# Turned rows and sums of values asked for at other steps in a fused stack of four graph attention layers

## The chip, the cores and the metric

The kernel runs on one core of a Trainium2 chip, in one launch. The metric is the device time of an execution in microseconds; the time of a kernel is the median of several executions. The engines of the core are named as in the profile: PE is TensorE (matmuls; PEld is its loading of weights), DVE is VectorE, ACT is ScalarE, POOL is GpSimd, and SP is SyncE, which only issues DMA transfers.

## The reference

3327 rows of 256 features pass through four layers over one adjacency matrix of 3327 x 3327 (0 or 1). Every layer is attention over the neighbours, a residual and a normalisation of rows:

```python
x = _layernorm(x + _L0_gnn_ref(x, adj, Wq, Wk))          # cosine attention on x itself
x = _layernorm(x + _L1_gnn_ref(x, adj, W, a))            # GAT: elu(att @ (x @ W))
x = _layernorm(x + _L2_gnn_ref(x, adj, Wq, bq, Wk, bk, Wv, bv))  # elu(softmax(q @ k.T / 16) @ v)
x = _layernorm(x + _L3_gnn_ref(x, adj, W0, W1, a1, W2, a2, W3, a3))  # x @ W0, then three GATs
```

with, for a GAT layer,

```python
h = x @ W
e = leaky_relu((h @ a[:D])[:, None] + (h @ a[D:])[None, :])
att = softmax(where(adj > 0, e, MASK_VAL), axis=1)
out = elu(att @ h)
```

## The kernel before

**Tiling.** The rows are padded to 3328, that is 26 row tiles of 128, and the columns of the attention matrix are cut into seven blocks: six of 512 (four row tiles each) and block 6 of 256 (two row tiles). The program has six stages, called layers in the code: "0", "1" (GAT), "2", and "3a", "3b", "3c" (the three GATs of the last layer). Its main loop runs over steps (layer, block b, row tile j). A step makes the attention weights e of row tile j against the columns of block b, and multiplies them with the values v of row tile j into the block's accumulators `po` in PSUM. After the 26 steps of a block, `finish` (L790) turns the accumulators into rows of the next layer.

**Weights.** In a GAT layer e comes from ScalarE (`re`, L599) and VectorE (L607) and needs no matmul. In layers "0" and "2" it needs the scores `ps` (TensorE, L444 and L506), an exponential (ScalarE, `ex`, L453 and L514) and the mask (VectorE, L433). Weights are made two steps ahead of their products (`LA = 2`), in five buffers. The mask of a block, 1664 KB in DRAM, is fetched at step j = 8 for the next block (L370), into two buffers; it can only be fetched when the last e that reads the old mask is made.

**Products.** Ordinarily they are one matmul for each group of 128 columns (L1163). In layer "2" and in blocks 1 to 5 of layer "0" they are done for pairs of row tiles with seven products in the manner of Strassen (L704). These use sums of weights (`ssum`, L645 on, VectorE) and sums of values, `tsum`: `combine` (L625) makes the sums of values of pair p once, on VectorE, and writes them to DRAM (`t_d`, 256 KB a pair, L636); `fetch_tsum` (L640, issued on SP at L642) brings them back into one of three buffers when a pair's weights are made. In layer "2" the values themselves are only made while layer "1" ends and layer "2" begins: those of row tiles 24 and 25 (pair 12) last, because the mean of all rows goes into the very last one (`Sum.close`, L783).

**Turned rows.** A GAT projects its rows after the attention, for which TensorE needs them transposed. `turn` (L752) does so: ScalarE copies the rows into two planes of 16-bit halves (`planes`, L759), SP issues a DMA transpose (`turned`, L762), and after `steps` yields VectorE copies the halves to their places (L769). Then come the projections `pproj` (L924) on TensorE, ELU (ScalarE L937 and L938, VectorE L944 and L953), statistics (L802, L803), the reciprocal square root `rsqrt` (L132 to L144, eleven small operations on VectorE), and the normalised rows o (L982). In layer "1" those are written to DRAM (`x_d`, L994) and turned a second time, into `FT`; from FT TensorE makes layer 2's values with `pv` (L1011), and `combine` follows. FT is also what layer 2's scores read. `block2` (L458) prepares a block of layer 2's scores: `pgq` (L465), `gT` (L472), its largest magnitudes gm (L480), a sum over partitions `pn` (L488), and from that, by another rsqrt, a bound `off` (L496).

**Order.** `finish` is a generator. It is advanced once a step (`advance`), and what is left of it at j = 20 is flushed, so each `yield` spreads its work over one more step of the next block. The rows of block 5 are thus worked on during block 6, whose steps are about half as long, and those of block 6 in the first block of the next layer. The first four steps are laid down in the order written; from there on a scheduler orders the instructions of each engine by its own model of time, with the order of emission as priority. On each engine instructions then run in that order.

## Time and profile before

| | |
|---|---|
| time, median of 3 runs | 2385.57 us (2384.24 to 2386.73) |
| the profiled execution's own time | 2386.53 us |
| its span | 2384.5 us |
| TensorE's granted clock, mean | 0.996 of full speed |
| DMA, mean | 89 GB/s |
| `turned`: DVE idle until the transpose has landed | 26.2 us in 32 waits |
| `tsums`: fetches | 156, of 256.5 KB |
| mask fetches of 1664 KB | 30 |

The span reaches from the first to the last instruction that the profiler saw; the execution's own time has 2.0 us around it. A wait is idle time of an engine together with what ended it. Idle time of an engine that doesn't set the pace costs nothing by itself: VectorE's 26.2 us before the turned rows are only of account where TensorE stops in turn. In a line of the timeline the first two columns are start and duration in us, then engine, line, operation, output<-inputs, and how many instructions of the kind run there; a bracket gives the idle time ahead of it and what ended that.

### The profile page before, as it was taken

To read this page: it belongs to the slowest core of one execution; us is meant where nothing else is said; L and a number is where in the kernel's file an instruction comes from. 1 tells how busy PE (TensorE), PEld (TensorE's weight loads), DVE (VectorE), ACT (ScalarE), POOL (GpSimd) and SP (SyncE) were. 2 spreads that over 40 slices of the span, in tenths; PEclk is the share of its full clock that TensorE was granted. 3 is DMA by queue.
4 is the path that set the end of the run, shared out by engine and by line. 5 is a ranking of instruction groups with operands and counts; after the bars stand their busy time and mean duration, and the time that the engine had idled before them with its cause. 6 is when DMAs were issued, how large, how long until landed. Compare 5 with 4: busy or idle time off the path is not lost.

```text
span 2384.5 us, 33058 instructions
## 1 busy us (share of the span) xinstructions
PE 2348.6 (98%) x11911; PEld 1915.7 (80%) x11911; DVE 1615.5 (68%) x4340; ACT 1215.7 (51%) x1982; POOL 14.2 (1%) x91
## 2 busy tenths in 40 slices
PE   9999999999999999999999999999999999999997
PEld 6687777888888776667767798888888888888886
DVE  7789999866676657567567585556656555655665
ACT  5666666665555422222222255565655555655554
POOL 0000000000000000000000000000000000000000
PEclk9999999999999999999999999999999999999999
DMA  7556555523222322212212221221211111132121
GB/s 230 169 164 193 187 183 185 164 89 87 73 75 64 102 54 91 73 59 87 72 51 73 78 92 47 67 56 31 73 49 43 43 59 50 45 98 69 60 61 27
DMA packets 146233, 212.83 MB, mean 89 GB/s; under 512 B 76062, under 2 KB 100885, under 8 KB 141461
## 3 DMA queue, kind: packets, MB, share of 16 engines
q1 hardware_dynamic: 145796, 210.45, 29.3%
q8 instruction: 94, 1.54, 0.3%
q14 instruction: 71, 0.57, 0.1%
q10 hardware_dynamic: 272, 0.26, 0.1%
HBM read 165.70 MB, written 28.19 MB: 81 GB/s over the span
## 4 chain that ended last, share of the span: by engine, by line
PE 64%; DVE 2%; DMA 1%; ACT 1%; issue 0%; DVEq 0%; POOL 0%; POOLq 0%; SPq 0%; ACTq 0%
PE po L1163 37%; PE ps L506 12%; PE po L704 11%; PE pproj L924 3%; PE pgq L465 1%; DMA turned<-planes 1%; ACT re L599 1%; DMA t_d<-tsum 0%; PE pv L1011 0%; DVE e L607 0%; DVE ejunk L533 0%; DVE pT L769 0%; ACT planes L759 0%; DMA u<-s_d 0%; DVE v L953 0%
## 5 line engine op out<-in xcount | busy, mean ns | idle before, releaser
L1163 PE MATMUL po<-v,e 128*128 128x257 f32 x5720 | 1275.7, 381 | 2.8 <-ACT p L882 2.0
L1163 PEld LDWEIGHTS po<-v,e 128*128 128x128 f32 x5720 | 1083.2, 190 | 178.1 <-issue 14.6
L599 ACT ACTIVATE re<-u,nrh,th 128x512 f32<-128x512 f32 (+1 forms) x728 | 558.8, 783 | 488.6 <-DVE e L607 485.8
L607 DVE SCALAR_TENSOR_TENSOR e<-re,rh,mask 128x512 f32<-128x512 f32 (+1 forms) x728 | 515.1, 711 | 389.5 <-PE po L1163 366.3
L433 DVE SCALAR_TENSOR_TENSOR e<-ex,mask 128x512 f32<-128x512 f32 (+1 forms) x364 | 236.5, 655 | 183.0 <-ACT ex L514 156.7
L506 PE MATMUL ps<-gT,ft 128*128 128x512 f32 (+1 forms) x728 | 307.7, 563 | 0.0
L514 ACT ACTIVATE ex<-ps,off 128x512 f32<-128x512 f32 (+1 forms) x182 | 119.4, 657 | 360.3 <-PE ps L506 332.3
L704 PE MATMUL po<-tsums,ssum 128*128 128x128 f32 (+1 forms) x1794 | 250.1, 275 | 3.0 <-DMA tsums<-t_d 1.6
L704 PEld LDWEIGHTS po<-tsums,ssum 128*128 128x128 f32 x1794 | 224.4, 192 | 5.4 <-DMA tsums<-t_d 2.4
L704 PEld LDWEIGHTS po<-v,e 128*128 128x128 f32 x1196 | 169.7, 191 | 71.6 <-issue 54.3
L506 PEld LDWEIGHTS ps<-gT,ft 128*128 128x128 f32 x728 | 131.9, 190 | 113.6 <-issue 110.7
L704 PE MATMUL po<-v,e 128*128 128x129 f32 x1196 | 183.2, 275 | 0.2 <-DVE e L433 0.2
L453 ACT ACTIVATE ex<-ps 128x512 f32<-128x512 f32 (+1 forms) x182 | 102.9, 565 | 119.3 <-PE ps L444 107.3
L444 PE MATMUL ps<-ft,ft 128*128 128x512 f32 (+1 forms) x312 | 142.9, 566 | 0.8 <-ACT ft L356 0.7
L405 DVE CUSTOM_DVE_ANT_0 acc<-acc,stage 128x1024 uint16<-128x1024 uint16 (+1 forms) x168 | 111.5, 663 | 13.0 <-DMA stage<-in_adj_a 8.3
L704 PE MATMUL po<-v,ssum 128*128 128x128 f32 x598 | 92.3, 275 | 0.0
L704 PE MATMUL po<-tsums,e 128*128 128x128 f32 x598 | 92.2, 275 | 0.0
L397 ACT ACTIVATE mask<-pos 128x1024 uint8<-128x1024 bf16 (+1 forms) x87 | 86.6, 995 | 2.4
L396 ACT ACTIVATE pos<-stage 128x1024 bf16<-128x1024 int32 (+1 forms) x87 | 85.8, 987 | 2.7 <-DVE e L433 2.7
L924 PE MATMUL pproj<-w_l_w,pT 128*128 128x256 f32 x312 | 80.2, 381 | 3.8 <-DVE pT L769 2.2
L704 PEld LDWEIGHTS po<-v,ssum 128*128 128x128 f32 x598 | 79.4, 192 | 0.1
L704 PEld LDWEIGHTS po<-tsums,e 128*128 128x128 f32 x598 | 79.3, 192 | 0.1
(191 smaller groups left out, 1667.9 us busy)
## 6 DMA issues: line engine op xcount, KB each, us to landing
mask<-mask_d SPq DMA_DIRECT2D x30, 1664.0 KB
tsums<-t_d SPq DMA_DIRECT2D x156, 256.5 KB
stage<-in_adj_a SPq DMA_DIRECT2D x78, 512.0 KB
mask_d<-mask SPq DMA_DIRECT2D x6, 1664.0 KB
t_d<-tsum SPq DMA_DIRECT2D x26, 256.5 KB
u<-s_d SPq DMA_DIRECT2D x24, 256.0 KB
mask<-mask_d SPq DMA_DIRECT2D x5, 832.0 KB
v<-in_x SPq DMA_DIRECT2D x26, 128.0 KB
```

The source lines that it names most:

```text
L397: nc.scalar.activation(mask(b, j, 2), t_[:, : 2 * wd], AF.Sign)
L405: nc.vector.tensor_tensor(acc, acc, st[:, h * wd : (h + 1) * wd], ALU.add)
L433: nc.vector.scalar_tensor_tensor(e[:, :wd], t_[:, :wd], 0.0, mask(b, j), ALU.add, ALU.mult)
L444: nc.tensor.matmul(ps[:, :wd], FT[j // 4][:, 0, (j % 4) * P : (j % 4 + 1) * P], FT[b][:, 1, :wd], start=True, stop=True,)
L453: nc.scalar.activation(t_[:, :wd], ps[:, :wd], AF.Exp)
L506: nc.tensor.matmul(ps[:, :wd], FT[j // 4][:, h, (j % 4) * P : (j % 4 + 1) * P], g[:, h, :wd], start=(h == 0), stop=(h == 1),)
L514: nc.scalar.activation(t_[:, :wd], ps[:, :wd], AF.Exp, bias=off, scale=1.0 / D**0.5)
L599: nc.scalar.activation(t_[:, :wd], self.u[b][:, :wd], AF.Relu, bias=self.nrh[:, j : j + 1], scale=self.th[:, j : j + 1],)
L607: nc.vector.scalar_tensor_tensor(e[:, :wd], t_[:, :wd], self.rh[:, j : j + 1], mask(b, j), ALU.add, ALU.mult,)
L704: nc.tensor.matmul(o, x, y, start=(p == 0 and g not in banks[:i]), stop=(p == NT // 2 - 1 and g not in banks[i + 1 :]),)
L924: nc.tensor.matmul(pm[:, :D], pT[:, h, :], w[L.w][:, h, :], start=(h == 0), stop=(h == 1),)
L1163: nc.tensor.matmul(pos[k], es[:, k * P : (k + 1) * P], V[L.i % 2][j], start=(j == 0), stop=(j == NT - 1),)
```

## The change

Sums of values are fetched for the pair at hand and for the one two steps later, with a fourth buffer; pair 12 of layer 2's block 0 is left out of the early fetch. `turn` waits four steps by default instead of three; a GAT's first turn waits seven for block 5's rows instead of five; layer 1's second turn waits six for block 5's rows and four otherwise, instead of three. To make room, two tiles of the start (`count`, `part`) and the mean's row share buffers that other tiles use at other times.

```diff
-    count = const.tile([P, P], F32, name="count")
+    count = work.tile([P, P], F32, tag="sq0", name="count", bufs=1)
...
-    part = const.tile([P, P], F32, name="part")
+    part = work.tile([P, P], F32, tag="sq1", name="part", bufs=1)
...
     def fetch_tsum(key, b, p):
-        t = work.tile([P, 4 * H + 1], F32, tag="tsum", name="tsums", bufs=3)
+        t = work.tile([P, 4 * H + 1], F32, tag="tsum", name="tsums", bufs=4)
...
-    def turn(x4, n, out, steps=3):
+    def turn(x4, n, out, steps=4):
...
         def close(self, v):
...
-            row = work.tile([P, D], F32, tag="mrow", name="mrow", bufs=1)
+            row = work.tile([P, D], F32, tag="elu_e", name="mrow", bufs=2)
...
                     lambda t: pT4[:, :n].bitcast(U16).rearrange(
                         "p k h (i t) -> p t k h i", t=2
                     )[:, t],
-                    5 if b == NB - 2 else 3,
+                    7 if b == NB - 2 else 4,
                 )
...
                     lambda t: FT[b].bitcast(U16).rearrange(
                         "p h (k i t) -> p t k h i", k=4, t=2
                     )[:, t, :n],
+                    6 if b == NB - 2 else 4,
                 )
...
+    fetched = set()
...
     def make(s):
         if s >= len(steps):
             return
         L, b, j = steps[s]
-        if strassen(L, b) and j % 2 == 0:
-            fetch_tsum(L.key, b, j // 2)
+        if j % 2 == 0:
+
+
+            for n in (s, s + 2):
+                if n < len(steps) and not (n > s and steps[n] == (layers[2], 0, NT - 2)):
+                    if strassen(*steps[n][:2]) and n not in fetched:
+                        fetch_tsum(steps[n][0].key, steps[n][1], steps[n][2] // 2)
+                        fetched.add(n)
```

## The prediction

> **What bounds the kernel now.** I read the page's shares of busy time first, then TensorE's list of waits, then the timeline around each wait that the change could touch.

> ```profile
> span 2384.5 us, 33058 instructions
> PE 2348.6 (98%) x11911; PEld 1915.7 (80%) x11911; DVE 1615.5 (68%) x4340; ACT 1215.7 (51%) x1982; POOL 14.2 (1%) x91
> L1163 PE MATMUL po<-v,e 128*128 128x257 f32 x5720 | 1275.7, 381 | 2.8 <-ACT p L882 2.0
> ```

> TensorE is busy for 98% of the span at full clock, and the change removes no matmul. So no edit can bring more than the waits it removes, and any edit can cost a new wait. The list of TensorE's waits (total, times, longest) says what is there to win:

> ```profile
> PE pproj L924 <- DVE pT L769: 3.1, 6, 0.7
> PE po L1163 <- ACT p L882: 2.0, 2, 1.3
> PE po L704 <- DMA tsums<-t_d: 1.6, 1, 1.6
> PE pv L1011 <- DVE ft L769: 1.0, 1, 1.0
> PE pn L488 <- DVE g L485: 0.5, 1, 0.5
> ```

> The edits aim at the first, third and fourth lines: 3.1 + 1.6 + 1.0 = 5.7 us, 0.24% of the span. Everything else they could do is loss. From the timeline, the six waits of pproj are 0.32 at 749.4 us and 0.28 at 1612.8 (ordinary blocks), and 0.71 at 801.1, 0.59 at 1709.9, 0.60 at 2029.3 and 0.59 at 2348.9 (last blocks of layers 1, 3a, 3b, 3c). The one wait of pv is where layer 1 gives over to layer 2. I show that place, all engines, because my forecast hangs on it:

> ```profile
> 813.06 1.38 DVE L982 TENSOR_SCALAR o<-y,st,rstd 128x256 f32<-128x256 f32 x4
> 814.52 1.99 ACT L759 COPY planes<-o 128x1024 uint16<-128x1024 uint16 x2 [0.75 <-DVE o L982]
> 816.54 1.94 SPq L762 DMA_TRANSPOSE turned<-planes  x1
> ...
> 819.16 0.36 SPq L370 DMA_DIRECT2D mask<-mask_d  x1
> ...
> 820.87 1.36 DVE L769 COPY ft<-turned 128x1024 uint16<-128x1024 uint16 x2 [0.51 <-DMA turned<-planes]
> ...
> 822.37 3.69 PE L1011 MATMUL pv<-w_l_wvt,ft 128*128 128x256 f32 x16 [0.99 <-DVE ft L769]
> ```

> It reads as one chain: normalise block 5's rows (o), split them into planes, transpose by DMA (4.33 us from issue to the first copy), copy out, and only then can TensorE form layer 2's values. The chain is already 0.99 us late with the mask issued *behind* the transpose.

> The stall for sums of values, SP's row of issues:

> ```profile
> 915.43 0.34 SPq L370 DMA_DIRECT2D mask<-mask_d  x1
> 915.87 0.37 SPq L636 DMA_DIRECT2D t_d<-tsum  x1
> 916.29 2.06 SPq L887 DMA_DIRECT2D x<-x_d  x4
> 925.19 1.27 SPq L642 DMA_DIRECT2D tsums<-t_d  x3
> ```

> The fetch at 925.19 waited until the write of 915.87 had landed, 9.3 us later, behind a 1664 KB mask. It is late because pair 12 of layer 2's block 0 is *written* late.

> [...] ready matmuls of `ps` (layer 2's scores) stand behind the waiting pv and don't pass it. [...] a 256 KB write took 9.3 us behind a mask. [...]

> **The change part by part.** Emission order only gives priorities here; a scheduler puts the instructions in place. So I take moves from the instruction order that the changed kernel is built to, and durations from before.

> *Sums two pairs ahead, fourth buffer.* Of 156 fetches one stalled TensorE, 1.58 us. It is the fetch for pair 12 of layer 2's block 0, which the edit exempts, and SP's order around it is the same in both kernels. Gain 0; the other 155 already had cover. Cost: none seen, the number of transfers is the same. *count, part and mrow in shared buffers:* 0, they live at the start and at a layer's end only, and the mean's row waits there for nothing that TensorE needs.

> *One more step for pT (3 to 4), ordinary blocks.* DVE's copies keep their place, the pproj behind them come a step later: the waits of 0.32 and 0.28 go, −0.6. pv gets two more steps, and its sixteen matmuls stand in one clump instead of two; the DVE clump that follows (values, sums, about 5.2 us without an e) is covered by the five e buffers: a step is eight matmuls of 0.22 us (24 took 5.36), so four full buffers behind the one in use are 7.1 us of work. Cost 0; up to 1 us a block, 5 in all, if that cover fails.

> *Seven steps instead of five for block 5's rows.* These are worked on during block 6, whose steps are short (four matmuls of 0.23 us, 0.9 us). In the built order pT's copies stay behind the same e, and the first pproj stays behind the first matmul of row tile 10, as before. So 0.71, 0.59, 0.60, 0.59 stay. What moves are the later pproj: they stand behind row tiles 10, 11, 13, 15 instead of 10, 10, 11, 13. In 3a to 3b this changes nothing (0.63 stays). In 3b to 3c ScalarE no longer has the exponential of u, which waited for its DMA, ahead of p: −0.7 of the 1.32.

> *The same in layer 1: the new wait.* The last pproj was over at 807.7. It now has one more row tile and the first pgq (1.9 us) ahead of it, and ends near 811.05. The statistics of the last rows end near 812.95 (before: 810.57, 2.8 us after the pproj; the added third is pproj's delay less a wait of DVE for it). Before, the eleven operations of rsqrt then ran with one e between them, and o came at 813.06. Now VectorE's built order mixes them with the other chain of that place, the bound of layer 2's scores: the reduction gm (1.21 us), its small operations, n (which waits for TensorE's pn), and the e of row tiles 20 to 25. Counted on from 812.95 at the durations of before: var and three rsqrt operations 0.75, gm 1.21 (its gT is there by 813.8), g at 816.7, pn 816.9, n 817.75, then nine small ones at 0.17 to 0.2 and two e at 0.48 to rstd and the last e at 820.4, and four o at 0.35 with three small ones between: last o at 822.5 instead of 814.44. Planes 2.0 us: transpose issued at **824.5 instead of 816.54**. SP's order turns too: the mask's fetch, which waits for the last e (820.4), and four 128 KB writes of x_d now stand *ahead* of the transpose.

> Bounds for the landing: with no crossing 824.5 + 4.33 = 828.9. [...] 1664 + 512 KB, at the mask's 1664 KB in about 4.9 us (its packets of 819.16 ran until 825.1), from 822 on end at 828.4, and the transpose's own 1.94 makes 830.3. Copies 1.4: pv starts between 830.3 and 831.7, I take 831.0. TensorE is through with all of layer 1's products by then: 821.38 (its stop in before) + 1.37 (row tiles 24 and 25, which before stood behind pv, six matmuls of 0.23) + 0.35 (pn later, 816.9 for 816.55) = 823.1. Nothing can fill: pv is at the head, ps behind it. **New stall 7.9 us in place of 0.99; with pn +7.3.** Behind pv nothing else is late: the first e of layer 2 was ready 8.8 us after pv's start, and TensorE now has pv and 16 matmuls of ps, 11.2 us, ahead of its user.

> *Layer 3c's end:* x lands near 2368.5, needed at 2369.2; 0, with 0.5 either way.

> Sum: +7.3 − 0.6 − 0.7 = **+6.0 us** on a profiled execution of 2386.53 (span 2384.5 and 2.0 around it), which lies 1.0 above the median of 2385.57. On the median: 2391.6. What a measurement of this kernel can tell from no change is about 0.2%, 4.8 us, so 2380.8 to 2390.3.

> **The rivals.**
> - *A, it does what it is written for.* More steps take the waits away and no chain gets late. For: the 0.6 of ordinary blocks does go. Against: the rows of block 5 are bound at TensorE's end, where no step is left to give. It decides if the transpose of 816.5 is issued by 817.7, so that pv is not over 1 us later than TensorE. Then −0.6 − 0.7 − up to 1 − up to 2.5 (last blocks): 2381 to 2384.5. This one ends on the other side.
> - *B, it doesn't do what it says.* The scheduler undoes the steps and the one late fetch is exempt, and DVE's mixing costs only a little: 2385 to 2388. For: in the last blocks the copies have not moved. Against: the built order at 811 us has.
> - *C, worse.* The late chain also drags the writes of t_d (4.3 us from issue before) and with them the e behind them on VectorE, and ordinary blocks lose cover: stall 11 and up to 5 more: 2395 to 2400. For: VectorE waited 3.39 us for such a write at 829.9. Against: TensorE has 11.2 us of work there.

> **How the numbers follow.** Forecast 0.69, own range 2389.5 to 2394; A 0.08; B 0.13; C 0.10. Range 2386 to 2396 leaves out A, some of B, most of C. Faster 0.05 (A's lower part and unknowns), same 0.22 (rest of A, B, the low edge of the forecast), slower 0.73.

> **What would show it.** In the changed kernel's waits of TensorE: pv <- DVE ft about 8 us, pproj <- pT about 2.5, tsums <- t_d still near 1.6, po <- p about 1.3. In the timeline at 820 us the mask's issue ahead of the transpose, and o ending after 820. I am wrong if pv waits under 4 us there (VectorE's order costs less than counted, or TensorE was late itself), or if the ordinary blocks show new waits for e.

## The result and the profile after

The changed kernel takes 2395.45 us (median of six, 2394.76 to 2398.28), the kernel before 2386.43 us on the same chip: 9.0 us more, a ratio of 1.0039 (95% interval 1.0028 to 1.0050). The forecast was 2391.6 us in a range of 2386 to 2396. The profiled execution took 2395.00 us with a span of 2393.2 us; the kernel before had 2386.53 and 2384.5.

The page, as far as it answers to the lines shown of before:

```profile
span 2393.2 us, 33056 instructions
PE 2348.8 (98%) x11911; PEld 1917.3 (80%) x11911; DVE 1613.3 (67%) x4340; ACT 1214.2 (51%) x1982; POOL 13.5 (1%) x91
```

The number of matmuls is the same (11911), and the span is 8.7 us longer. TensorE's busy time is the same too, to 0.2 us (2348.6 before), so the page has TensorE standing still for longer. That equal busy time hides something: a matmul at a lowered clock counts as busy for longer (pv, below: 6.12 us for 3.69). The changed kernel has about 4 us of that behind two of its waits (2.4 and 1.6, below); the kernel before ran at half clock (0.50) from 100.6 to 107.4 us, where the changed kernel kept 1.00. TensorE's list of waits (total, times, longest) says where:

```profile
PE pv L1012 <- DVE ft L769: 9.1, 1, 9.1
...
PE pproj L924 <- DVE pT L769: 2.9, 4, 1.1
...
PE po L704 <- DMA tsums<-t_d: 1.9, 1, 1.9
...
PE po L1171 <- ACT p L882: 1.0, 2, 0.5
...
PE pn L488 <- DVE rs_q L141: 0.4, 1, 0.4
```

The wait that has grown, from 1.0 to 9.1 us, is pv, at the change from layer 1 to layer 2. The two short waits of pproj in ordinary blocks are gone (six waits became four), p has lost 1.0, tsums still waits once. Now the timeline of that place:

```profile
816.43 0.33 SPq L370 DMA_DIRECT2D mask<-mask_d  x1
...
816.82 2.35 SPq L994 DMA_DIRECT2D x_d<-o  x4
...
817.57 0.40 DVE L982 TENSOR_SCALAR o<-y,st,rstd 128x256 f32<-128x256 f32 x1
...
818.05 1.99 ACT L759 COPY planes<-o 128x1024 uint16<-128x1024 uint16 x2 [3.59 <-DVE rs_q L142]
...
820.07 5.59 SPq L762 DMA_TRANSPOSE turned<-planes  x1
...
827.77 1.37 DVE L769 COPY ft<-turned 128x1024 uint16<-128x1024 uint16 x2 [7.24 <-DMA turned<-planes]
...
829.19 6.12 PE L1012 MATMUL pv<-w_l_wvt,ft 128*128 128x256 f32 x16 [9.06 <-DVE ft L769]
```

The order has turned: the mask (816.43) is issued ahead of the four writes of x_d (816.82 on) and of the transpose (820.07). The writes stood ahead of the transpose in the kernel before as well (813.50 there), so only the mask's place is new. From the transpose's issue to VectorE's first copy it now takes 7.70 us, where it took 4.33. The packets in the two traces, told apart by their sizes, show where it went: before, those of the transpose ran from 817.7 to 820.4 and the mask's from 820.2 on; now the mask's ran from 817.4 to 824.0, x_d's from 822.8 to 825.4 and the transpose's from 824.2 to 827.2. TensorE was through with layer 1 at 820.13 and waited; the scores ps, behind pv in its order, started at 835.15, with the last of pv. And one line reads differently from what the list of waits can tell: the same sixteen matmuls of pv take 6.12 us instead of 3.69. The granted clock (the number behind POOL's) says why. A line has a stretch from:to, its length, the busy time of PE, PEld, DVE, ACT and POOL with counts, the granted clock, the DMA share and GB/s:

```profile
820.00:829.10 9.10, 0.13 (x1) 0.00 (x0) 1.75 (x5) 0.96 (x3) 0.58 (x1) 0.71 0.82 218
829.10:832.00 2.90, 2.81 (x7) 2.28 (x8) 0.63 (x3) 0.00 (x0) 0.00 (x0) 0.50 0.00 0
832.00:835.00 3.00, 3.00 (x11) 2.45 (x10) 1.67 (x6) 0.00 (x0) 0.00 (x0) 0.65 0.00 0
```

The clock is lowered from 823.8 to 834.1 us, so after the wait TensorE runs at half clock for 4.9 us and counts as busy in it. So the wait costs its 9.06 us and 2.4 us more behind it.

Where the span's 8.7 us come from, by the starts of the same instructions in both traces (us):

| stretch | before | after | difference |
|---|---|---|---|
| start to first pproj of layer 1's last block | 801.08 | 798.64 | −2.44 |
| from there to the seventh matmul of layer 2's first products | 33.65 | 44.04 | +10.39 |
| from there to the products that wait for tsums | 93.19 | 93.52 | +0.33 |
| from there to the first pproj of 3a's last block | 781.94 | 782.99 | +1.05 |
| from there to the first pproj of 3c's last block | 639.08 | 638.15 | −0.93 |
| from there to the end of the span | 35.56 | 35.86 | +0.30 |

The second line is pv: +8.1 of wait and +2.4 of clock, together 10.5. The fourth holds another 1.6 us of lowered clock after the wait for tsums, less the 0.28 of an ordinary block and some tenths. The first line is mostly no effect of the change: by 155 us the changed kernel's trace is 1.6 us ahead, and the other ten of this study stand between 2.4 us ahead of the one of before and 4.1 us behind it.

### The profile page after: what moved, and what is told of

Read it like the earlier page. It is cut to its first block, busy times and chain, and to the rows that moved or that the text cites. A ratio compares the mean times of both kernels' runs of the same rounds, so it can differ in the third digit from the quotient of the medians.

```text
span 2393.2 us, 33056 instructions
## 1 busy us (share of the span) xinstructions
PE 2348.8 (98%) x11911; PEld 1917.3 (80%) x11911; DVE 1613.3 (67%) x4340; ACT 1214.2 (51%) x1982; POOL 13.5 (1%) x91
## 4 chain that ended last, share of the span: by engine, by line
PE 88%; DVE 7%; DMA 3%; ACT 1%; issue 0%; SPq 0%; DVEq 0%; ACTq 0%
PE po L1171 49%; PE po L704 16%; PE ps L506 12%; PE pproj L924 4%; PE ps L444 3%; DVE e L433 1%; DMA t_d<-tsum 1%; PE pv L1012 1%; DVE acc L405 1%; PE pgq L465 1%; DMA stage<-in_adj_a 1%; DVE ejunk L533 1%; DMA turned<-planes 1%; PE pqk L311 0%; DVE ssum L654 0%
## 5 line engine op out<-in xcount | busy, mean ns | idle before, releaser
L704 PE MATMUL po<-tsums,ssum 128*128 128x128 f32 (+1 forms) x1794 | 251.2, 276 | 3.3 <-DMA tsums<-t_d 1.9
L704 PEld LDWEIGHTS po<-tsums,ssum 128*128 128x128 f32 x1794 | 225.4, 193 | 5.7 <-DMA tsums<-t_d 2.7
L704 PEld LDWEIGHTS po<-v,e 128*128 128x128 f32 x1196 | 169.7, 191 | 71.3 <-issue 54.1
L704 PE MATMUL po<-v,e 128*128 128x129 f32 x1196 | 183.2, 275 | 0.0
L704 PE MATMUL po<-tsums,e 128*128 128x128 f32 x598 | 92.6, 276 | 0.0
L704 PE MATMUL po<-v,ssum 128*128 128x128 f32 x598 | 92.4, 275 | 0.0
L924 PE MATMUL pproj<-w_l_w,pT 128*128 128x256 f32 x312 | 80.6, 381 | 3.9 <-DVE pT L769 2.3
L704 PEld LDWEIGHTS po<-tsums,e 128*128 128x128 f32 x598 | 79.8, 193 | 0.0
L704 PEld LDWEIGHTS po<-v,ssum 128*128 128x128 f32 x598 | 79.6, 193 | 0.1
```

Source lines behind the costliest of these rows:

```text
L704: nc.tensor.matmul(o, x, y, start=(p == 0 and g not in banks[:i]), stop=(p == NT // 2 - 1 and g not in banks[i + 1 :]),)
L924: nc.tensor.matmul(pm[:, :D], pT[:, h, :], w[L.w][:, h, :], start=(h == 0), stop=(h == 1),)
```

## The experiments

Each comparison had the kernel before beside it on the same chip; ratios are to that. Experiments 1 to 4 are one comparison, 5 to 7 another, and 8 a third with `five_again`.

**1. One number put back** (`l1_five`, run again as `five_again`).

```diff
-                    7 if b == NB - 2 else 4,
+                    (5 if L.key == "1" else 7) if b == NB - 2 else 4,
```

> The changed kernel with one number put back: in layer 1, block 5's rows wait five steps at the first turn instead of seven; every other edit stays. My theory (the two added steps there push the last pproj behind the first pgq, mix the two rsqrt chains on VectorE and put the mask ahead of the transpose): TensorE's wait of pv falls from 9.1 us to about 1, pv lasts 3.7 us instead of 6.1, and the time to 2383.5 to 2386.5, that is 0 to 3 us under the kernel before, for the waits of pproj in ordinary blocks and of p that the rest removes. Rival (the second turn's six steps, or the early fetches, move the work): pv still waits 8 to 10 us and the time stays at 2393 to 2397.

Measured: 2385.66 us beside 2386.56, ratio 0.9993 (0.9987 to 1.0000).

> The same kernel as l1_five, beside the one before it in this list on the same chip: within 1 us of the kernel before, on its lower side, and 1 to 2 us over the other if the theory there holds.

Measured again: 2385.91 beside 2387.43, ratio 0.9993 (0.9984 to 1.0001). The waits in the trace of `l1_five`:

```profile
PE pproj L924 <- DVE pT L769: 2.9, 4, 1.1
...
PE po L704 <- DMA tsums<-t_d: 1.5, 1, 1.5
...
PE pv L1012 <- DVE ft L769: 1.0, 1, 1.0
```

The wait of pv is back at 1.0 us, and pv takes 3.69 us. What is left is the sum of the small gains, 1.7 us by the ratio, at the edge of what can be told from nothing.

**2. The same number alone, in the kernel before** (`l1_seven`).

```diff
-                    5 if b == NB - 2 else 3,
+                    (7 if L.key == "1" else 5) if b == NB - 2 else 3,
```

> The kernel before with one number changed: in layer 1, block 5's rows wait seven steps at the first turn instead of five. My theory: this alone brings the whole loss, pv waits 8.5 to 9.5 us, runs 6.1 us, and the time is 2395 to 2398, 9 to 11 us over the kernel before. Rival (the loss needs the other edits too): pv waits under 3 us and the time is within 2 us of the kernel before.

Measured: 2395.03 us beside 2386.56, ratio 1.0035 (1.0022 to 1.0048); pv waits 9.24 us and takes 5.85:

```profile
829.11 5.85 PE L1011 MATMUL pv<-w_l_wvt,ft 128*128 128x256 f32 x16 [9.24 <-DVE ft L769]
```

With the first experiment this makes those two steps in layer 1 both necessary and sufficient for the loss.

**3. The second turn put back** (`second_three`).

```diff
-                    6 if b == NB - 2 else 4,
+                    3,
```

> The changed kernel with layer 1's second turn put back to three steps in all blocks (instead of six for block 5's rows and four otherwise). My theory: the second turn comes after the damage, so pv still waits 8.5 to 9.5 us and the time is that of the changed kernel within 1.5 us (2394 to 2397). Rival (the later copy out into FT is what pv waits for): pv waits about 1 us, 2384 to 2387.

Measured: 2396.14 us, ratio 1.0035 (1.0021 to 1.0049); pv waits 8.89 us and takes 6.37:

```profile
834.68 6.37 PE L1012 MATMUL pv<-w_l_wvt,ft 128*128 128x256 f32 x16 [8.89 <-DVE ft L769]
```

The rival falls: the later copy into FT is not what pv waited for.

**4. The mask behind the transpose** (`mask_behind`). The mask's buffer first gets one byte of FT from VectorE, so its fetch can only be issued after FT is copied out.

```diff
-    def fetch_mask(b):
+    def fetch_mask(b, after=None):
         m = new_mask(b)
+        if after is not None:
+            nc.vector.tensor_copy(m[:, 0:1], after.bitcast(U8)[:, 0:1])
...
-            masks[nb] = fetch_mask(nb)
+            masks[nb] = fetch_mask(nb, FT[NB - 2][:, 0, 0:1] if (L.key, b) == ("2", 0) else None)
```

> The changed kernel, with the mask's fetch for layer 2's block 1 made to wait until FT of block 5 has been copied out, so that the transpose is issued and served ahead of it; nothing is left out. My theory (the transpose stood in its ring behind the mask): from the transpose's issue to VectorE's first copy takes 4.3 to 5 us instead of 7.7, pv waits 5.5 to 6.5 us instead of 9.1, the time is 2391 to 2393. Rival (the transpose is slow in itself at that place, or the four writes of x_d alone hold it up): 7 us or more from issue to copy, pv waits about 9 us, 2395.

Measured: 2391.92 us beside 2386.56, ratio 1.0022 (1.0013 to 1.0032). Its timeline:

```profile
821.91 1.79 SPq L996 DMA_DIRECT2D x_d<-o  x4
...
825.15 1.96 SPq L764 DMA_TRANSPOSE turned<-planes  x1
829.45 1.35 DVE L771 COPY ft<-turned 128x1024 uint16<-128x1024 uint16 x2 [3.84 <-DMA turned<-planes]
...
830.86 6.50 PE L1014 MATMUL pv<-w_l_wvt,ft 128*128 128x256 f32 x16 [5.64 <-DVE mask L371]
830.87 0.32 SPq L372 DMA_DIRECT2D mask<-mask_d  x1
```

From issue to copy it is 4.30 us again. So the mask ahead in the queue cost 3.4 us, and nearly all of the rest of the wait, 5.64, is o coming late. The x_d writes are still ahead in order, but their last packet ended at 824.7, before the transpose was issued; what they cost by themselves when they stand behind the mask is not shown. The clock fell in this run too (0.50 from 831 to 834 us, and pv took 6.50).

**5. TensorE kept busy** (`filler`). Sixteen matmuls that nobody reads stand ahead of pv.

```diff
+                if b == NB - 2:
+                    fl = bank("fill")
+                    for i in range(16):
+                        nc.tensor.matmul(fl[:, :D], o4[:, 3, :P], o4[:, 3, :], start=True, stop=True)
```

> The changed kernel with sixteen more matmuls (thirty-two in the trace, about 7.4 us) whose results nobody reads, put ahead of pv in layer 1's last block; they need only o, so they run while TensorE would wait for the transpose. If the 2.4 us by which pv ran longer in the changed kernel came from a clock that fell because TensorE stood still, pv lasts 3.7 us instead of 6.1, the granted clock stays at 1.0 there, and the time falls by about 2.4 us to 2392 to 2394. If pv was slow for another reason (its operands, the transfers beside it), it stays near 6 us and the time is the changed kernel's or longer, 2395 to 2398.

Measured: 2391.63 us beside 2384.75, ratio 1.0032 (1.0021 to 1.0044).

```profile
819.17 7.17 PE L1004 MATMUL fill<-o 128*128 128x256 f32 x32
...
830.51 3.69 PE L1016 MATMUL pv<-w_l_wvt,ft 128*128 128x256 f32 x16 [1.99 <-DVE ri L878]
```

The transpose is as late as in the changed kernel (7.78 us from issue to copy), but TensorE waits 1.99 us ahead of pv instead of 9.06, the granted clock is 1.00 from 812 to 845 us, and pv takes its 3.69 us. So the 2.4 us were the clock's, shown by doing *more* work. The interval of the time overlaps that of the changed kernel; the pv line carries the verdict.

**6. The early fetches alone** (`only_early_fetch`): steps 7, 4 and 6, 4 put back to 5, 3 and 3.

> The changed kernel with all steps of turned rows as before, so that only the early fetch of sums with its fourth buffer and the shared buffers are left. My theory: the one stalled fetch is exempt and the others had cover, so the time is that of the kernel before within 1 us (2385.5 to 2387.5), tsums still waits about 1.5 us once and pv about 1 us. Rival (the early fetches get in the way of other transfers, or bring the third line of the waits): 2 us or more either way.

Measured: 2385.92 us beside 2384.75, ratio 1.0004 (0.9996 to 1.0012); tsums waits 1.3 us once, pv 1.0. Nothing, as expected.

**7. Pair 12's write on ScalarE's queue** (`own_queue_five`, the changed kernel with five steps for layer 1's block 5), and the same with six steps (`own_queue_six`).

```diff
-        nc.sync.dma_start(t_d[key][p], t)
+        eng = nc.scalar if (key, p) == ("2", NT // 2 - 1) else nc.sync
+        eng.dma_start(t_d[key][p], t)
```

> The changed kernel with layer 1's block 5 at five steps, and the write of pair 12's sums issued by ScalarE instead of SP, so that it doesn't stand behind the mask's fetch, which waits on SP for the last e. Theory (SP's order, not the distance of the fetch, made that stall): the wait for tsums goes from 1.5 us to under 0.3, and the time is 1.5 us under the same kernel without this edit: 2383 to 2385. Rival (the landing itself is slow beside the mask): the wait stays over 1 us, 2385 to 2386.5.

Measured: 2386.06 us beside 2384.75, ratio 1.0006 (0.9997 to 1.0014). A miss: the wait for tsums *rose* to 2.7 us. The write was issued at 914.27 and the fetch could go at 921.64, 7.4 us later. The queue was another, but the mask issued at 914.02 had packets from 915.0 to 920.5, and the write's ran beside them, from 918.2 to 920.9. And the scheduler put pair 12's products earlier in TensorE's order, before the sums could be there.

> As the kernel before this one in the list, with six steps instead of five for layer 1's block 5. In the order it is built to, the pproj stand behind row tiles 10, 10, 12, 14, all ahead of the first pgq, the rows o come behind one chain of rsqrt that is not mixed with the other, and the mask stays behind the transpose. Theory (it is the crossing with pgq and the mask that costs, not a step as such): pv waits under 3 us and the time is within 2.5 us of the kernel with five. Rival (each step there costs its share of the loss): pv waits about 5 us and the time is 4 to 6 us longer than with five.

Measured: 2386.69 us beside 2384.75, ratio 1.0010 (1.0004 to 1.0017); pv waits 1.70 us, tsums 3.3. The transpose (815.43) is issued ahead of the mask (817.45) and lands after 4.30 us. So a sixth step does little harm, and the seventh flips the order. (The write's own queue, the other difference between this kernel and the changed one, plays its part 100 us later.)

**8. The mask out of pair 12's way** (`five_and_clear`): experiment 1 with the helper of experiment 4, where the mask for layer 2's block 2 waits for an e of block 1.

```diff
+            masks[nb] = fetch_mask(nb, made[-1][:, 0:1] if (L.key, b) == ("2", 1) else None)
```

> The changed kernel with layer 1's block 5 at five steps, and the mask's fetch for layer 2's block 2 made to wait for an e of block 1, so that the write and the fetch of pair 12's sums go ahead of it on SP and in its ring. Theory (these two stood behind 1664 KB): the write lands 2 to 4 us after its issue instead of 9.3, TensorE's wait for tsums falls from 1.5 us to under 0.3, and the time is 1 to 2 us under the same kernel without this edit: 2383 to 2385 where the kernel before takes 2386. Rival (the chain from the mean's row is late by itself, and the write's landing is not what counts): the wait stays over 1 us and the time doesn't move.

Measured: 2385.83 us beside 2387.43, ratio 0.9995 (0.9986 to 1.0003), no better than `five_again` in the same comparison.

```profile
917.01 0.34 SPq L638 DMA_DIRECT2D t_d<-tsum  x1
920.60 1.74 SPq L644 DMA_DIRECT2D tsums<-t_d  x4
```

The mechanism was right, the write is through after 3.6 us instead of 9.0 in `five_again`, and yet TensorE's wait fell only from 1.3 to 0.8 us. In TensorE's order the products of these sums have moved forward as well, ahead of matmuls of scores that stood before them: they start at 923.32, and in `five_again` at 928.71.

## Why the prediction was right, and where it was off

*The mechanism and its place held.* Experiments 1 and 2 show that the two steps in layer 1 bring the loss, experiment 3 clears the second turn, and the waits and timeline show the chain that the forecast described: last pproj behind pgq, mixed rsqrt chains on VectorE, the mask ahead of the transpose. (That the writes of x_d *now* stand ahead was misread: they did before.) How the mixing came from the later pproj was read from the orders and not tested apart. In the traces of both kernels VectorE's 4340 instructions ran line for line in the order that the program is built to.

*The size was too small by 3 us* (+6.0 forecast, +9.0 measured). The terms, counted from the first pproj of the last block (801.08 before, 798.64 after):

| step | forecast | measured |
|---|---|---|
| last pproj over | 10.0 | 10.2 |
| last o | 21.4 | 19.3 |
| transpose issued | 23.4 | 21.4 |
| from issue to VectorE's copy | 4.3 to 5.8 | 7.7 |
| pv starts | 29.9 | 30.55 |
| TensorE through with layer 1 | 22.0 | 21.5 |
| wait of pv | 7.9 | 9.06 |
| pv longer by the clock | 0 | 2.4 |

Two terms erred against each other. VectorE was 2 us faster than counted; among other things its small operations of different chains run as close as 0.08 us apart, where I charged each 0.17 to 0.2. And the transpose was slower in its queue than my upper bound of 5.8 us, which took mask, writes of x_d and transpose one after another; that was an estimate. It did not meet more of the mask than I had assumed: 2.7 us of the mask's packets had run when it was issued, for 2.5 in the forecast. But the packets of mask and x_d together ran for 8.0 us, where I had counted 6.4, and for the transpose I had taken the 1.94 us of SP's issue, while its packets ran for 2.6 us in the kernel before and for 3.1 now. Of the 3.4 us that the mask costs (experiment 4), 2.9 lie between the transpose's issue and its first packet. The 0.35 us for a later pn did not come: it waits 0.44 us, and 0.52 before. That the time stayed within the range owes something to luck: with VectorE as slow as I had counted it would have been near 2397.5, as an estimate from the 2395.45 and the 2.1 us of the second line of the table.

The term that was left out altogether is the clock, 2.4 us. The step that failed is the "New stall 7.9 us" that goes into the sum with nothing behind it: it priced a wait by its length alone. In the changed kernel's trace the clock is at 0.50 from 3.7 us into the wait on, and the price was there to be read in the trace of before, where it stood at 0.50 from 100.6 to 107.4 us, around the end of a start-up wait of 3.3 us at 101.9.

*The parts costed at nothing or small.* The early fetch: nothing, by experiment 6. The waits of 0.32 and 0.28: gone; no new wait for e came with pv's clump. The last blocks: 1.09, 0.58, 0.60, 0.60 for 0.71, 0.59, 0.60, 0.59; they stayed, with 0.4 more in layer 1 that I had not seen. p from 3b to 3c: 1.32 to 0.52, so −0.8 for −0.7. Layer 3c's end: ppT waits 0.86 for 0.57, within the half us left open. Without the crossing these gains are what experiment 1 shows.

*The rivals.* A and B fall with the result: the transpose was issued at 820.07, where A needed 817.7, and B had VectorE's mixing cost only a little, where experiment 2 puts 8.5 us on the steps in layer 1 alone. C's time, 2395 to 2400, is the one that was measured, but not by C's mechanism: VectorE did wait for a write of t_d again, 2.63 us at 838.41, and TensorE came to layer 2's first products at 842.01, right behind its scores, without a wait. The range held the time near its upper end.

No version came out clearly ahead of the kernel before. The one of experiment 1 lies 0.07% below the kernel before in both of its runs, and both intervals end at 1.

## What to carry to other kernels

Where rows are handed from one stage to the next at a stage's end, an added step of slack can be none: work that is moved back can cross work that was safely behind it, here a 1664 KB fetch ahead of a 512 KB transpose in one queue, 3.4 us by experiment 4. So compare the orders that the program compiles to on each engine and on the DMA queue, above all at boundaries. And price a long wait of TensorE with what comes after it: here 2.2 to 2.8 us of lowered clock for waits of 5.6 to 9.2 us, and 1.6 us for one of 1.90 (the last section says when). When an edit makes data come earlier, look whether the scheduler has moved its user earlier too.

## What the hardware showed that was not expected

The lowered clock. In the four traces with a wait of pv of 5.64 us or more, pv took 5.85 to 6.50 us; in those with a wait of up to 2.0 us it took 3.69. Between, the length alone doesn't decide: after the 1.90 us wait for tsums in the changed kernel the clock was 0.66 over the next 5 us and the products behind it took 1.6 us longer, and after one of 2.66 us (`own_queue_five`) it fell too (0.72 from 927 to 931 us), while after 3.29 us in the same place (`own_queue_six`) it stayed at 1.00.

```profile
933.10:936.50 3.40, 1.50 (x7) 0.67 (x7) 0.69 (x1) 0.39 (x1) 0.00 (x0) 1.00 0.55 180
936.50:939.90 3.40, 3.40 (x18) 3.40 (x17) 0.95 (x6) 0.00 (x0) 0.00 (x0) 0.50 0.38 135
```

and `own_queue_six` around its 3.29 us (920.7 to 923.9):

```profile
918.70:922.20 3.50, 1.96 (x7) 0.65 (x5) 2.87 (x8) 1.12 (x3) 0.00 (x0) 1.00 0.31 108
922.20:925.60 3.40, 1.65 (x14) 1.65 (x15) 0.00 (x1) 0.00 (x0) 0.00 (x0) 1.00 0.93 304
```

The number after the comma is the length, the next TensorE's busy time, and the third from the end the clock. The shorter wait fell whole into one step, which left TensorE busy for 0.44 of it, and the next step ran at half clock. The longer one was cut in two by the grid, each step kept 0.47 or more, and the clock stayed. Over all steps at full clock in the twelve traces, up to the last matmul: of those with TensorE busy for under 0.43 of the step, 20 of 20 were followed by half clock; between 0.43 and 0.46, 3 of 5; and of more than 8000 busier ones a single one, with 0.55. In the traces of the two kernels alone, the steps that half clock followed had 0.36 (before), 0.00 and 0.44 (changed), and every other 0.47 or more. That is a rule read from these traces, not one that an experiment set out to test. As an estimate from it, a wait of 3.9 us or more always leaves one step with less than 0.43 of work, wherever the grid lies, and a shorter one may or may not.
